# Graph attention, four layers on one core: elu and statistics on GpSimd, preparation spread over groups, stores apart

## The chip, the cores and the metric

The kernel runs on one core of one Trainium2 chip. The metric is the device time of one execution in microseconds, taken as the median of three: 2753.4 (2751.53 to 2755.9). Engines are named as in the profile: PE is TensorE, ACT is ScalarE, DVE is VectorE, POOL is GpSimd, SP issues most of the transfers.

## The reference

Sixteen batches of 1024 nodes with 256 features go through four layers of graph attention over one adjacency matrix. Each layer normalises its input, applies relu, projects it with W, and adds the attended result to x. Layers 0 and 2 have four heads of 64 features, layers 1 and 3 one head of 256. Layer 3 ends in relu, the others in elu.

```
h = maximum(layernorm(x), 0)            # eps 1e-5, over 256 features
Wh = h @ W                              # heads H, features D = 256 / H
e[i, j] = leaky_relu(Wh[i] . a_src + Wh[j] . a_dst)      # slope 0.2, layer 3: 0.01
alpha = softmax over j of (e where adj[i, j] > 0, else -inf)     # layers 2, 3: adj != 0
x = x + elu(alpha @ Wh)                 # layer 3: relu
```

All data are fp32.

## The kernel before

**The trick.** The exponential of a leaky relu of a sum is a maximum of two products of a factor of i and a factor of j. So no matrix of exponentials is computed. For a head, g is a row of 1024 factors of i, copied to all 128 partitions. One DVE instruction per 128 nodes j makes the tile w = max(g, rcol of j) x mask (L250, 128x1024, with g in PSUM and the mask as bytes in SBUF). TensorE multiplies w as the stationary operand with whx, the projected features scaled by the other factor, and a last column gives the softmax's divisor.

**Steps and groups.** The work is a list of 64 steps, each one layer on one batch (`order_of_steps`, L409). Four batches (streams) are under way at once and take turns, so that the next layer of a batch comes three or four steps later (two at the very end: step 61 is layer 2 of batch 15, step 63 its layer 3). A step has eight groups of aggregation. In a wide step (four heads) each head has eight tiles of w and two groups, each with four blocks of 128 nodes i. In a narrow step (one head) there are eight tiles in all, and each group has one block. `aggregate` (L254) emits a group's matmuls and one ACT copy of its PSUM sums to y (L270). PSUM has two buffers for these sums (`ps_acc`), two for g (`ps_g`), and two shared by transpositions and projections (`ps_p`).

**The order is written by hand.** From L387 on (`tc.manual_schedule()`) every engine gets its instructions in the order in which the Python program emits them. For group k of step n this is: the tiles that this head still lacks; the matmuls of the group and its y copy; pieces of the finish of step n-1 that are due; pieces of preparations that are due (`prepare`, L334); some tiles ahead (`emit_tiles`, L357): four per wide group, two per narrow one, never more than WBUFS = 19 beyond the last head that is done. The preparation of the first two steps stands ahead of this block (L383 to L385), where the framework's scheduler sets the order.

**Preparation of a step** (`preparation`, L149): statistics of 512 rows each (`stats`, twice: bn_stats and bn_aggr on DVE, then 1/sqrt and the shift on POOL), normalisation (`normalise`, four ACT copies each, twice), four transpositions (PE, then an ACT copy with relu), eight projections (two PE pairs each, three ACT copies; for wide layers a POOL product besides), the factors (`factors`, two ACT exponentials and a POOL minimum), and `rows`: a transposition of gcol, an ACT copy, and a transfer to DRAM. PREPARATION (L40) gives to each of these 18 pieces the group, counted from the start, in which it is due. A step's preparation starts two steps ahead, at group 0, or at group 4 where the last layer of the same batch is too near (L391).

**Tiles.** `fetch` (L236) reads a head's factors back from DRAM to all partitions (SP), `broadcast` (L242) copies them to PSUM on ACT (g), `weights` (L247) makes a tile. A head's g can be emitted once the whole preparation of its step has been emitted (`done["prepared"]`), and its place in ACT's queue is behind everything emitted before. If a step begins and its preparation isn't emitted yet, the rest of it is emitted on the spot (L362 to L367).

**Finish of a step** (`finish`, L272), in the next step: at group 0 the reciprocal of the divisor (DVE) and the scaling of the first half (POOL), at 1 that of the second half and the exponential of the first (ACT), at 2 and 3 the rest. `scaled` (L289) multiplies y and makes e = min(y, 0). `add` (L302) computes elu as max(e - 1, y) in one DVE instruction and adds it to x on POOL; in layer 3 one DVE instruction adds relu(y) to x, and the transfer of the half to DRAM is issued at once, with the load of the stream's next batch after the second. The tile e and the normalised tile xn share three buffers named t4.

Of the kernel before, what the change touches and what calls it, by code (L numbers as in the profile page):

```python
# [38 lines left out]
WBUFS = 19  # L39
PREPARATION = (0, 0, 1, 2, 3, 3, 4, 4, 5, 5, 5, 5, 6, 6, 7, 7, 8, 9)  # L40
# [11 lines left out]
def kernel(ctx: ExitStack, tc: tile.TileContext, x, adj, ws, avs, out):  # L52
# [96 lines left out]
    def preparation(n):  # L149
# [6 lines left out]
        def stats(half):  # L156
            if half == 0:
                st["mv"] = small.tile([P, C, 2], F32, name="mv")
                st["bn"] = small.tile([P, C, 6], F32, name="bn")
            for c in range(half * HALF, (half + 1) * HALF):  # L160
                nc.vector.bn_stats(st["bn"][:, c, :], xs[b][:, c, :])  # L161
                nc.vector.bn_aggr(st["mv"][:, c, :], st["bn"][:, c, :])  # L162
            if half == 1:
                rstd = st["rstd"] = small.tile([P, C], F32, name="rstd")
                nc.gpsimd.tensor_scalar(rstd, st["mv"][:, :, 1], EPS, None, op0=ALU.add)
                nc.gpsimd.tensor_tensor(rstd, rstd, neghalf, op=ALU.pow)  # L166
                shift = st["shift"] = small.tile([P, C], F32, name="shift")
                nc.gpsimd.tensor_tensor(shift, st["mv"][:, :, 0], rstd, op=ALU.mult)
                nc.gpsimd.tensor_scalar(shift, shift, -1.0, None, op0=ALU.mult)

        def normalise(half):
            xn = st["xn", half] = prep.tile([P, HALF, F], F32, name="t4", bufs=3)
# [61 lines left out]
        return list(zip(PREPARATION, out + [factors, rows], strict=True))  # L234
# [37 lines left out]
    def finish(n):  # L272
# [16 lines left out]
        def scaled(half):  # L289
# [3 lines left out]
            if l < L - 1:  # L293

                e = st["e", half] = prep.tile([P, HALF * H, D], F32, name="t4", bufs=3)
                nc.gpsimd.tensor_scalar(e, yh, 0.0, -3.0e38, op0=ALU.min, op1=ALU.max)  # L296
# [5 lines left out]
        def add(half):  # L302
            xh, yh, r = views(half)
            if l < L - 1:
                e = st["e", half]
                nc.vector.scalar_tensor_tensor(e, e, -1.0, yh, op0=ALU.add, op1=ALU.max)  # L306
                nc.gpsimd.tensor_add(xh, xh, e)  # L307
                return
            nc.vector.scalar_tensor_tensor(xh, yh, 0.0, xh, op0=ALU.max, op1=ALU.add)
            nc.sync.dma_start(  # L310
                out=out[b, half * HALF * P:(half + 1) * HALF * P, :].rearrange(
                    "(c p) f -> p c f", p=P), in_=xs[b][:, half * HALF:(half + 1) * HALF, :])
            if half == 1 and b + STREAMS < B:
# [4 lines left out]
                (2, lambda: add(0)), (3, lambda: add(1))]  # L318
# [12 lines left out]
    done = {"tiles": 0, "g": 0, "gs": 0, "free": 0, "prepared": 0, "wanted": 0}  # L331
    agenda = []

    def prepare(upto):  # L334

        while agenda and (agenda[0][0] <= upto or agenda[0][1] < done["wanted"]):
            _, n, piece, last = agenda.pop(0)
            piece()
            if last:
                done["prepared"] = n + 1  # L340
                fetch_heads()

    def plan(n, at):
# [101 lines left out]
```

## Time and profile before

The execution that was profiled took 2758.29 us, and its span, from the first instruction to the last, is 2756.5 us. That is 4.9 us over the median.

| what | us |
|---|---|
| median of three executions | 2753.4 |
| profiled execution | 2758.29 |
| its span | 2756.5 |
| matmuls of the aggregation (L266), busy | 1965.4 |
| matmuls of the projections (L195), busy | 515.8 |
| transpositions (L183), busy | 155.4 |
| tiles of w (L250), busy | 1543.3 |
| statistics bn_stats (L161), busy | 200.7 |

A group's row in the profile gives the line, the engine, the operation, the tiles written and read, their shapes, the number of instructions, then the busy time, the mean duration in ns, and the engine's idle time ahead of these instructions with what ended most of it. A line of waits gives who waited for whom: the sum in us, how often, and the longest. PEld is the load of stationary operands and runs beside PE; the ends of matmuls are modelled. Each L266 matmul stands in the trace as two records[...].

### The profile page before, as it was taken

What the parts mean: (1) busy time and instruction counts of PE and PEld (TensorE: products, weight loads), DVE (VectorE), ACT (ScalarE), POOL (GpSimd) and SP (SyncE); (2) the same over time, 40 slices, a digit from 0 to 9 for tenths busy, and PEclk for the clock granted to TensorE, in tenths of its full rate; (3) what the DMA queues carried; (4) which work ended last, traced back from release to release, by engine and by line L of the source; (5) the groups of instructions that cost most, each with busy time, mean ns of one, the idle gap of its engine ahead of it and who ended that gap; (6) DMA issues with size and microseconds to landing.
All of it is one profiled execution on the core that took longest, in us unless ns stands there. A gap on an engine that the chain in (4) does not pass through costs nothing.

```text
span 2756.5 us, 88771 instructions
## 1 busy us (share of the span) xinstructions
PE 2581.3 (94%) x40080; PEld 2268.5 (82%) x40080; DVE 1984.5 (72%) x2569; ACT 1199.6 (44%) x3265; POOL 896.6 (33%) x909
## 2 busy tenths in 40 slices
PE   1789988999999999999999999999999999999997
PEld 1688777888888888888888888888888888888876
DVE  5596855767966779747977679767797488775772
ACT  0534444444444444544444445444444444444341
POOL 0223333343332343342242343333323333433221
PEclk9999999999999999999999999999999999999998
DMA  4111010012211210111211111002112111101101
GB/s 138 62 49 40 10 40 25 25 36 67 72 36 44 71 49 25 41 39 47 88 41 48 62 40 41 33 17 71 56 49 71 34 46 64 34 17 39 56 25 39
DMA packets 63674, 130.08 MB, mean 47 GB/s; under 512 B 6208, under 2 KB 41792, under 8 KB 63296
## 3 DMA queue, kind: packets, MB, share of 16 engines
q1 hardware_dynamic: 60608, 123.35, 13.4%
q8 instruction: 315, 5.16, 0.8%
q10 hardware_dynamic: 2688, 1.05, 0.2%
q14 instruction: 63, 0.52, 0.1%
HBM read 106.95 MB, written 17.43 MB: 45 GB/s over the span
## 4 chain that ended last, share of the span: by engine, by line
PE 72%; DVE 14%; DMA 6%; ACT 4%; issue 3%; POOL 1%; DVEq 0%; ACTq 0%; SPq 0%; POOLq 0%
PE acc L266 53%; PE pp L195 15%; DVE w L250 11%; DMA gs<-grow 4%; PE pp L183 3%; DMA grow<-gT 2%; DVE bn L161 1%; ACT t L300 1%; ACT g L245 1%; DVE t L306 1%; DVE mv L162 1%; ACT whx L197 1%; DMA a_bc<-in_L_gnn_a 1%; ACT whx L201 0%; ACT y L270 0%
## 5 line engine op out<-in xcount | busy, mean ns | idle before, releaser
L266 PE MATMUL acc<-whx,w 128*64 128x65 f32 x36864 | 1965.4, 242 | 77.9 <-DVE w L250 56.9
L266 PEld LDWEIGHTS acc<-whx,w 128*64 128x64 f32 x36864 | 1764.3, 145 | 265.5 <-DVE w L250 78.7
L250 DVE SCALAR_TENSOR_TENSOR w<-g,rcol,mask 128x1024 f32<-128x1024 f32 x1280 | 1543.3, 1273 | 523.4 <-ACT g L245 432.7
L270 ACT ACTIVATE y<-acc 128x260 f32<-128x260 f32 (+1 forms) x512 | 196.8, 384 | 1071.1 <-PE acc L266 1069.8
L195 PE MATMUL pp<-wx,hT 128*128 128x258 f32 (+1 forms) x2048 | 515.8, 395 | 2.9 <-ACT hT L184 2.7
L291 POOL TENSOR_TENSOR y<-y,r 128x1024 f32<-128x1024 f32 x128 | 243.0, 1899 | 716.1 <-DVE r L287 716.1
L195 PEld LDWEIGHTS pp<-wx,hT 128*128 128x128 f32 x2048 | 378.3, 192 | 78.1 <-ACT hT L184 15.7
L307 POOL TENSOR_TENSOR x<-x,t 128x1024 f32<-128x1024 f32 x96 | 226.8, 2362 | 408.2 <-DVE t L306 399.6
L206 POOL TENSOR_TENSOR whx<-whx 128x256 f32<-128x256 f32 x256 | 157.5, 618 | 471.2 <-ACT whx L204 471.2
L175 ACT ACTIVATE t<-x,shift,rstd 128x256 f32<-128x256 f32 x512 | 264.8, 588 | 78.7 <-POOL x L307 56.6
L245 ACT ACTIVATE g<-gs 128x1024 f32<-128x1024 f32 x160 | 163.5, 1022 | 129.5 <-DMA gs<-grow 128.0
L197 ACT ACTIVATE whx<-pp,nbias 128x4 f32<-128x4 f32 (+1 forms) x512 | 135.5, 265 | 181.3 <-PE pp L195 169.7
L161 DVE BATCH_NORM_STATS2 bn<-x 128x6 f32<-128x256 f32 x512 | 200.7, 392 | 2.4 <-DMA x<-in_x 2.4
L183 PE MATMUL pp<-ident,t 128*128 128x128 f32 x1024 | 155.4, 284 | 34.0 <-ACT t L175 18.9
L183 PEld LDWEIGHTS pp<-ident,t 128*128 128x128 f32 x1024 | 111.3, 141 | 78.8 <-ACT whx L201 28.0
L184 ACT ACTIVATE hT<-pp 128x512 f32<-128x512 f32 x256 | 145.5, 593 | 19.2 <-PE pp L183 18.8
L306 DVE SCALAR_TENSOR_TENSOR t<-t,y 128x1024 f32<-128x1024 f32 x96 | 118.4, 1233 | 35.4 <-ACT t L300 35.3
L287 DVE RECIPROCAL r<-y 128x32 f32<-128x32 f32 (+1 forms) x64 | 17.6, 276 | 160.0 <-ACT y L270 159.9
L201 ACT ACTIVATE whx<-pp,whx 128x256 f32<-128x256 f32 x256 | 121.7, 475 | 0.0
L166 POOL TENSOR_TENSOR rstd<-rstd,neghalf 128x8 f32<-128x8 f32 x64 | 106.7, 1668 | 5.3
L162 DVE BATCH_NORM_AGGREGATE mv<-bn 128x2 f32<-128x6 f32 x512 | 92.8, 181 | 16.9
L296 POOL TENSOR_SCALAR t<-y 128x1024 f32<-128x1024 f32 x96 | 101.7, 1060 | 8.5
(37 smaller groups left out, 533.0 us busy)
## 6 DMA issues: line engine op xcount, KB each, us to landing
gs<-grow SPq DMA_DIRECT2D x160, 512.0 KB
x<-in_x SPq DMA_DIRECT2D x16, 1024.0 KB
out<-x SPq DMA_DIRECT2D x32, 512.0 KB
a_raw<-in_adj SPq DMA_DIRECT2D x8, 512.0 KB
a_bc<-in_L_gnn_a ACTq DMA_DIRECT2D x8, 128.0 KB
wx<-in_L_gnn_W SPq DMA_DIRECT2D x4, 256.0 KB
grow<-gT SPq DMA_DIRECT2D x32, 16.0 KB
grow<-gT SPq DMA_DIRECT2D x32, 4.0 KB
```

The source lines that it names most:

```text
L161: nc.vector.bn_stats(st["bn"][:, c, :], xs[b][:, c, :])
L175: nc.scalar.activation(xn[:, q, :], xs[b][:, c, :], AF.Identity, bias=st["shift"][:, c:c + 1], scale=st["rstd"][:, c:c + 1])
L183: nc.tensor.transpose(pt[:, q, :], st["xn", half][:, q, k * P:(k + 1) * P], ident)
L195: nc.tensor.matmul(pw, lhsT=st["hT", half][:, k, q * P:(q + 1) * P], rhs=wx[l][:, k, :], start=(k == 0), stop=(k == K - 1))
L197: nc.scalar.activation(whx[:, c, :, D], pw[:, F + H:F + 2 * H], AF.Exp, bias=nbias[l], scale=slope)
L206: nc.gpsimd.tensor_tensor(whx[:, c, :, 0:D], whx[:, c, :, 0:D], whx[:, c, :, D:D + 1].to_broadcast([P, H, D]), op=ALU.mult)
L245: nc.scalar.activation(g, state[n]["gs", h], AF.Copy)
L250: nc.vector.scalar_tensor_tensor(w, state[n]["g", h], state[n]["rcol"][:, jc, h:h + 1], masks[LAYERS[steps[n][1]][3]][:, jc, :], op0=ALU.m ...
L266: nc.tensor.matmul(acc[o % P:o % P + cols, q, :], lhsT=st["w", h, jc][:, o:o + cols], rhs=st["whx"][:, jc, h, :], start=(jc == 0), stop=(j ...
L270: nc.scalar.activation(st["y"][:, i0:i0 + per, h, :], acc, AF.Copy)
L291: nc.gpsimd.tensor_tensor(yh, yh, r[:, :, None].to_broadcast([P, HALF * H, D]), op=ALU.mult)
L307: nc.gpsimd.tensor_add(xh, xh, e)
```

## The change

The change has these parts:

- `stats` no longer calls bn_aggr. The means and squared deviations of the even and the odd elements that bn_stats leaves are combined for all 1024 rows at once by ten small POOL instructions (there were four).
- In `add`, elu's last step moves from DVE to POOL: y becomes max(y, 0) - 1, then e + y, then x + e.
- xn and e have buffers of their own, two each, and WBUFS goes from 19 to 18.
- A preparation has 20 pieces. Its last one does nothing but mark it as done, two groups after `rows` and the fetch of the first heads. PREPARATION spreads the pieces over 14 groups (it was 10). BEGIN and L394 to L402 of the new text give the start: two steps ahead, three groups earlier for wide steps; never before group 5 of the step in which the last layer of the same batch is finished (group 0 of the step after it for layer 0, whose x must be loaded first); and at least three groups after the one before it.
- The first two preparations are emitted inside the hand-written order.
- Where a preparation is late, the pieces of all steps that are due up to its end are emitted.
- In layer 3 both halves' stores, and the load after them, are issued at group 4 of the next step.

```diff
-WBUFS = 19
-PREPARATION = (0, 0, 1, 2, 3, 3, 4, 4, 5, 5, 5, 5, 6, 6, 7, 7, 8, 9)
+WBUFS = 18
+PREPARATION = (0, 1, 3, 4, 5, 5, 6, 6, 7, 7, 7, 7, 8, 8, 9, 9, 10, 11, 11, 13)
+BEGIN = {1: 0, 4: -3}
...
             for c in range(half * HALF, (half + 1) * HALF):
-                nc.vector.bn_stats(st["bn"][:, c, :], xs[b][:, c, :])
-                nc.vector.bn_aggr(st["mv"][:, c, :], st["bn"][:, c, :])
+                nc.vector.bn_stats(bn[:, c, :], xs[b][:, c, :])
             if half == 1:
+                m0, s0, m1, s1 = (bn[:, :, i] for i in (1, 2, 4, 5))
                 rstd = st["rstd"] = small.tile([P, C], F32, name="rstd")
-                nc.gpsimd.tensor_scalar(rstd, st["mv"][:, :, 1], EPS, None, op0=ALU.add)
+                nc.gpsimd.tensor_tensor(dev, m0, m1, op=ALU.subtract)
+                nc.gpsimd.tensor_tensor(dev, dev, dev, op=ALU.mult)
+                nc.gpsimd.tensor_scalar(dev, dev, 0.25, EPS, op0=ALU.mult, op1=ALU.add)
+                nc.gpsimd.tensor_tensor(rstd, s0, s1, op=ALU.add)
+                nc.gpsimd.tensor_scalar(rstd, rstd, 1.0 / F, None, op0=ALU.mult)
+                nc.gpsimd.tensor_tensor(rstd, rstd, dev, op=ALU.add)
                 nc.gpsimd.tensor_tensor(rstd, rstd, neghalf, op=ALU.pow)
...
-            xn = st["xn", half] = prep.tile([P, HALF, F], F32, name="t4", bufs=3)
+            xn = st["xn", half] = prep.tile([P, HALF, F], F32, name="xn")
...
-        return list(zip(PREPARATION, out + [factors, rows], strict=True))
+        out += [factors, rows, lambda: fetch_heads(n + 1), lambda: None]
+        return [(begin[n] + k, piece) for k, piece in zip(PREPARATION, out, strict=True)]
...
-                e = st["e", half] = prep.tile([P, HALF * H, D], F32, name="t4", bufs=3)
+                e = st["e", half] = prep.tile([P, HALF * H, D], F32, name="e")
...
-                nc.vector.scalar_tensor_tensor(e, e, -1.0, yh, op0=ALU.add, op1=ALU.max)
+                nc.gpsimd.tensor_scalar(yh, yh, 0.0, -1.0, op0=ALU.max, op1=ALU.add)
+                nc.gpsimd.tensor_add(e, e, yh)
                 nc.gpsimd.tensor_add(xh, xh, e)
                 return
             nc.vector.scalar_tensor_tensor(xh, yh, 0.0, xh, op0=ALU.max, op1=ALU.add)
+
+        def store(half):
             nc.sync.dma_start(
...
-                (2, lambda: add(0)), (3, lambda: add(1))]
+                (2, lambda: add(0)), (3, lambda: add(1))] + (
+                    [(4, lambda: store(0)), (4, lambda: store(1))] if l == L - 1 else [])
...
-                    done["wanted"] = n + 1
-                    prepare(-1)
+                    prepare(max(a[0] for a in agenda if a[1] == n))
...
+        begin.append(8 * (n - 2) + BEGIN[LAYERS[l][0]] if n > 1 else -99)
+        if b % STREAMS in last:
+            begin[n] = max(begin[n], 8 * (last[b % STREAMS] + 1) + (8 if l == 0 else 5))
+        if n > 2:
+            begin[n] = max(begin[n], begin[n - 1] + 3)
...
-    for n in range(2):
-        plan(n, -99)
-        prepare(0)
     ending = []
     with tc.manual_schedule():
+        for planned in (1, 2):
+            plan(planned - 1)
+            prepare(-1)
...
-                if n + 2 < len(steps) and k == (0 if ready_at[n + 2] < n - 1 else 4):
-                    plan(n + 2, 8 * n + k)
+                while planned < len(steps) and begin[planned] <= 8 * n + k:
+                    plan(planned)
+                    planned += 1
```

## The prediction, made before the changed kernel was run

> **What bounds the kernel now.** I read the page's busy times first, then the waits, then the stretches, one per step of the schedule. "Wide" is a step with four heads (32 tiles of w), "narrow" one with a single head (8 tiles); n.k is group k of step n. "T" is a transposition, "P" a projection; 16.3 means step 16, group 3.
>
> ```profile
> PE 2581.3 (94%) x40080; PEld 2268.5 (82%) x40080; DVE 1984.5 (72%) x2569; ACT 1199.6 (44%) x3265; POOL 896.6 (33%) x909
> ...
> L307 POOL TENSOR_TENSOR x<-x,t 128x1024 f32<-128x1024 f32 x96 | 226.8, 2362 | 408.2 <-DVE t L306 399.6
> ...
> L306 DVE SCALAR_TENSOR_TENSOR t<-t,y 128x1024 f32<-128x1024 f32 x96 | 118.4, 1233 | 35.4 <-ACT t L300 35.3
> ...
> L162 DVE BATCH_NORM_AGGREGATE mv<-bn 128x2 f32<-128x6 f32 x512 | 92.8, 181 | 16.9
> L296 POOL TENSOR_SCALAR t<-y 128x1024 f32<-128x1024 f32 x96 | 101.7, 1060 | 8.5
> ```
>
> TensorE is busy 94% of the span: 175 us of idle are all there is to win, and 64 of these lie in the first 100 us, before the matrices have arrived. The waits say what VectorE lacks:
>
> ```profile
> DVE w L250 <- ACT g L245: 432.7, 38, 26.9
> ...
> ACT t L175 <- POOL x L307: 56.6, 15, 5.0
> ```
>
> VectorE, at 72%, is idle for lack of a broadcast g, not of time. Now the steps, cut where the last y copy of each starts (columns: stretch, its length, then the busy us of PE, PEld, DVE, ACT, POOL):
>
> ```profile
> 382.40:432.10 49.70, 38.10 (x1034) 35.09 (x1033) 49.43 (x56) 14.61 (x31) 13.18 (x11) 0.93 0.08 24
> 477.60:530.70 53.10, 45.80 (x1074) 41.24 (x1074) 48.27 (x55) 21.45 (x53) 13.19 (x11) 0.94 0.07 23
> 814.00:855.30 41.30, 41.09 (x1074) 37.79 (x1074) 38.56 (x46) 18.75 (x51) 6.37 (x7) 1.00 0.20 67
> 1051.40:1096.20 44.80, 41.89 (x1074) 38.23 (x1074) 42.57 (x50) 19.54 (x52) 16.88 (x17) 1.00 0.05 15
> ```
>
> They are the wide steps 6, 8, 16 and 22. Step 16 is entered with 12 tiles made, and TensorE never waits. Steps 6 and 8 are entered with six, and VectorE, busy all through step 6, sets the pace: 49.7 and 53.1 us. So the time is decided by how many tiles exist when a wide step begins. Floors, the shortest steps in this cut: wide 41.2, narrow 37.6. Steps 9 to 59 take 2056.9 together, 49 over their floors. What a step costs when it is entered with nothing stands near the end:
>
> ```profile
> 2657.76 0.27 PE L223 MATMUL pp<-ident,gcol 128*8 128x128 f32 x1
> ...
> 2658.17 0.25 ACT L225 ACTIVATE gT<-pp 8x128 f32<-8x128 f32 x1
> ...
> 2658.44 0.30 SPq L227 DMA_DIRECT2D grow<-gT  x1
> 2659.74 0.34 SPq L239 DMA_DIRECT2D gs<-grow  x1
> 2663.87 1.03 ACT L245 ACTIVATE g<-gs 128x1024 f32<-128x1024 f32 x1 [3.49 <-DMA gs<-grow]
> ...
> 2664.94 9.63 DVE L250 SCALAR_TENSOR_TENSOR w<-g,rcol,mask 128x1024 f32<-128x1024 f32 x8 [7.16 <-ACT g L245]
> ```
>
> From the transposition of the factors to the eighth tile: 16.8 us. Tiles stand 1.20 apart (9.63 for eight).
>
> **What the Trainium skill says.** "GPSIMD Engine Reference", 4.1 Engine selection: two-input elementwise work is about twice as slow on GpSimd, one-input work about line rate. The trace agrees: 2362 ns for L307 against 1233 for L306, and 1060 for the one-input L296. "SBUF — State Buffer", SBUF: two separate sides: GpSimd and VectorE exclude each other only where VectorE reads two SBUF operands or is in a two-port mode; w takes g from PSUM, so I give it no penalty, and its pitch in this trace is 1.20 in busy and idle stretches of GpSimd alike. "Perfetto Trace Analysis", Tensor Engine Instruction: ScalarE, VectorE and GpSimd are strict FIFO. That decides here: a g behind a y copy waits for TensorE.
>
> **The change, part by part.**
>
> Engines. VectorE loses 96 L306 (118 us) and 512 L162, of which a step shows a pitch of 0.53 per chunk going to 0.40: 1.1 us per step, 3.6 with the two L306. GpSimd gains per half one one-input operation (1.06) and one two-input (at most 2.36): 96 x 3.4 = 328 us, and six tiny ones per step (0.2 to 0.25, pitch 0.3): 1.8 x 64 = 115. It comes to some 1340 us, 48%. Its chain after a step is 2 x 2.95 (scale, clamp) + 2 x 5.8 (elu, add) = 17.5 us, plus 4.4 of statistics; x is complete some 24 us into the next step, while the earliest statistics of a wide step follow at group 5, 29 or more us in. I take 0 for it; if the cover is gone, see the rivals. That xn and e have buffers of their own takes the 56.6 us off ScalarE; behind them stand y copies, and TensorE's share is the 0.4 to 1.4 us by which narrow steps exceed 37.6. It is inside the 49.
>
> Spreading. The last piece of a preparation now lies 13 groups after its start, and g may be broadcast only after it. Counting the order of instructions: wide steps of layer 0 (16, 19, 21, 32, 35, 37, 48, 51, 53) start their preparation at group 0 two steps before, so the first g comes at group 5 of the narrow step ahead, not at group 1, and six tiles are issued before they begin. Wide steps of layer 2 keep 12. In steps 3, 5, 6, 8, 62 and 63 the preparation isn't over when the step begins: the rest is issued on the spot, ahead of its first matmul.
>
> (a) Start. The first two preparations now come under the written order. In the trace the first g (96.50) runs before the second preparation is done; in the new order of ScalarE it follows all of it. One preparation alone: eight normalisations (4.1) and the rest as in the trace from hT (74.2) to the factors' transposition (88.6), some 14. Statistics are ready 1.7 later (six more tiny operations). So 72.0 + 18 = 90, 108 for the second, gT and g: first w at 110 in place of 97.6, +12.5. Through step 1 VectorE is the bound: two L306 (2.4), half of step 3's statistics moved behind the last needed tile (2.6) and the missing aggregations (1) return 6. Net +6.
>
> (b) Steps 2 to 8. A forced entry in detail, step 6: after the last matmul of step 5, two P and two T stand ahead of the factors' transposition (3.8), then 16.8 to the eighth tile: 20.6. TensorE has P and T for 7.2 and its first group's 3.8 meanwhile: 10 lost. Then 24 tiles and half of the statistics, 28.8 + 1.6, set the end of step 6: 51 for the last tile, 7 more for its groups, 58. By the same working, a head's first group held until its eighth tile, steps 2 to 8 take 52.8, 45.6, 48.8, 56.0, 58.0, 42.6, 61.3 = 365.1; in the trace they are 50.6, 38.0, 42.2, 51.1, 49.7, 45.5, 53.1 = 330.2. Some 5 us of projections are put off beyond step 8 as well. +40.
>
> (c) Steps 9 to 59. Work only moves between neighbours; stalls count. Step 16: its first eight tiles are made as it begins; 24 more, a whole set of statistics (3.2), r, and about 2 us in which g stands behind a normalisation bring the last at 34.1. Without stalls TensorE needs it at 28.9 (six groups of 3.82, P and T 5.1, a quarter group): 5.3. Step 19 has another half of statistics ahead: 6.9. Step 21 has two sets, its first eight tiles come 2.8 late (g at 20.5 stands behind two P), and only 6 us of P and T lie in it: last tile at 37.6 against 25: 12.6. Sum 24.8 per round of 16 steps; three rounds and steps 14, 30 and 46 (1.5 each: they keep 12 tiles) make 79; less the 49 now: +30.
>
> (d) Steps 60 to 63. In the trace step 63 starts its preparation at 61.4, ahead of the finish of step 61 on the same batch; now at 62.5, after it. Step 62: 1.6 (y, factors) + 16.8 + 0.5 = 18.9 for a group of 3.5, so 43.3 with seven more. Step 63: normalisation to factors, with nothing beside it, 18.3; then 16.8 and a last pair: 35.8 + 24.4 = 60.2. Step 60 holds no P now (28.2), step 61 as before (40.8). 172.5 against 157.8, with 2 us of P moved ahead: +17. The last stores only change their place in SP's queue: 0; those of the other batches come one group later, still four groups, some 18 us, ahead of the next statistics of that stream: 0.
>
> Sum: 6 + 40 + 30 + 17 = +93 on the profiled 2758.3 (span 2756.5 and 1.8 around it). That execution is 4.9 over the median, so 2753.4 + 93 = 2846.
>
> **Rivals.** (1) Tiles suffice: the nine layer-0 entries cost 2 each, since step 16's last tile is only 5 behind and the 2 us of g and part of the rest may vanish; 79 becomes 22, total +36: 2789. For it: VectorE's 28% idle. Against: steps 6 and 8. (2) Faster: VectorE's relief decides. If the eight tiles of a forced entry were ready in the 11 us that TensorE still has work, not after 20, (a) and (b) would give 0, the 3.6 us would take 45 of the 49, the end would cost 17: 2725. Against: the 7.2 us from transposition to first tile are one row of DMA and copies that the change doesn't shorten. (3) GpSimd becomes the bound: statistics of a wide step, two groups after the elu, wait in VectorE's queue with all tiles behind them; 3 us at 28 wide steps is +84 on top: 2930. For it: 5.8 us per half in place of 3.6 (1.2 + 2.4); against: a margin of about 5 us and 52% idle.
>
> **How the numbers follow.** Forecast 0.63 (own range 2816 to 2876), rival 1 0.20, rival 2 0.07, rival 3 0.08, nothing to tell (within 0.2%, about what a measurement of this kernel can tell) 0.02. The range 2770 to 2890 holds the forecast and rival 1, and leaves out rivals 2 and 3. Unknown costs: elu operations 0 to +84, entries 2 to 9 each, start +3 to +10. Faster 0.07, same 0.02, slower 0.91.
>
> **What would show it.** First w near 110 us; about 20 us without accumulation ahead of steps 3, 5, 6, 8, 62 and over 30 ahead of 63; wide steps 16, 19, 21 at 46 to 50 us with VectorE busy throughout; VectorE down to about 1775 busy, GpSimd near 1340; no wait of L175's line for x. It would be wrong if those wide steps stay at 41 us, or if the statistics wait for GpSimd's x.

## The result: 6.2% slower, 77 us more than forecast

The changed kernel takes 2923.4 us, median of four executions (2921.1 to 2929.7), against 2754.7 us for the kernel before (2751.5 to 2756.4) on the same chip. The ratio is 1.0617, with a 95% interval of 1.0598 to 1.0637. The forecast was 2846, in a range of 2770 to 2890: the right sign, and a time outside the range.

Cut as in the prediction, where the last y copy of each step starts, the two profiled executions compare as follows. The forecast column adds the working on record to the stretch before.

| stretch | before | forecast | after | difference, forecast | difference, measured |
|---|---|---|---|---|---|
| steps 0 and 1 | 200.4 | 206.4 | 207.6 | +6 | +7.2 |
| steps 2 to 8 | 330.3 | 365.1 | 369.1 | +40 (5 of it later) | +38.8 |
| steps 9 to 59 | 2056.9 | 2086.9 | 2154.5 | +30 | +97.6 |
| steps 60 to 63 | 157.7 | 172.5 | 176.7 | +17 (2 of it earlier) | +19.0 |

The last column adds up to the difference of the spans (2918.9 less 2756.5) within 0.2 us. The forecast put 7 us of projections, which (b) and (d) count, into the middle. In the traces 24 records of projections move there, some 6 us (steps 2 to 8 have 233 of them in place of 249, steps 60 to 63 have 64 in place of 72). Counted like the forecast, (a) is 7 us for 6, (b) 43 for 40 and (d) 21 for 17. Term (c), the long middle, is 92 for 30, three times what was said. So the question is what happens in steps 9 to 59.

The page's busy times of the kernel after, then rows of its groups (line, engine, operation, tiles, shapes, count, then busy us, mean ns and the idle time before):

```profile
PE 2636.9 (90%) x40080; PEld 2310.4 (79%) x40080; DVE 1790.9 (61%) x1961; ACT 1209.5 (41%) x3265; POOL 1529.1 (52%) x1485
```

```profile
L319 POOL TENSOR_SCALAR y<-y 128x1024 f32<-128x1024 f32 x96 | 348.9, 3634 | 3.4
...
L320 POOL TENSOR_TENSOR e<-e,y 128x1024 f32<-128x1024 f32 x96 | 209.2, 2179 | 24.7 <-ACT whx L208 16.0 <-ACT e L313 1.4
...
L309 POOL TENSOR_SCALAR e<-y 128x1024 f32<-128x1024 f32 x96 | 99.8, 1040 | 8.5
```

VectorE is down to 1791 us, as forecast (1775). GpSimd stands at 1529 in place of 1340, and one row shows why: elu's max/add (L319) takes 3634 ns. The forecast gave it 1.06 us, from the row of the other one-input operation on the same shape (L309, 1040 ns here).

The waits of the kernel after, in the whole span (who waits for whom: us in total, times, longest):

```profile
DVE w L263 <- ACT g L258: 948.9, 97, 49.6
...
PE acc L279 <- DVE w L263: 126.0, 126, 7.8
DVE bn L164 <- POOL x L321: 81.7, 14, 16.0
...
PE pp L234 <- POOL gcol L229: 48.7, 20, 7.2
```

VectorE now waits 949 us for a broadcast g; before it was 433. It has less to do and gets its work later. Of the last two lines the first is new: statistics wait for GpSimd's x, which the forecast had named as a sign that it would be wrong. The other wait has grown from 3.0 us: TensorE itself stands before the transposition of the factors (L234) until GpSimd has taken their minimum (L229).

How that second wait arises is seen in step 15, in the order of time (start, us, engine, line, operation, then in brackets the idle time and who ended it):

```profile
840.86 0.31 ACT L227 ACTIVATE gcol<-sd,rbias 128x32 f32<-128x32 f32 x1
...
841.36 3.63 POOL L319 TENSOR_SCALAR y<-y 128x1024 f32<-128x1024 f32 x1
845.07 2.16 POOL L320 TENSOR_TENSOR e<-e,y 128x1024 f32<-128x1024 f32 x1
847.32 2.34 POOL L321 TENSOR_TENSOR x<-x,e 128x1024 f32<-128x1024 f32 x1
849.74 0.29 POOL L229 TENSOR_SCALAR gcol<-gcol 128x32 f32<-128x32 f32 x1
...
850.09 0.39 PE L234 MATMUL pp<-ident,gcol 128*32 128x128 f32 x1 [7.22 <-POOL gcol L229]
...
860.77 1.04 ACT L258 ACTIVATE g<-gs 128x1024 f32<-128x1024 f32 x1
861.84 8.43 DVE L263 SCALAR_TENSOR_TENSOR w<-g,rcol,mask 128x1024 f32<-128x1024 f32 x7 [35.45 <-ACT g L258]
```

The factors are ready at 841.17. A minimum of 0.29 us stands behind one half of elu in GpSimd's queue, and starts 8.6 us later. TensorE does nothing for 7.2 us before the transposition, since the aggregation stands behind it in TensorE's queue. And g for the wide step 16, which begins at 868.9, reaches VectorE after 35 us without work.

The steps 15, 16, 19, 21 and 22 of the kernel after (stretch, its length, then the busy us of PE, PEld, DVE, ACT, POOL, then TensorE's granted clock, the share of the DMA engines and GB/s):

```profile
822.10:868.90 46.80, 39.34 (x178) 33.40 (x179) 11.36 (x17) 17.68 (x50) 29.50 (x27) 0.93 0.11 35
868.90:916.70 47.80, 44.63 (x1075) 40.76 (x1074) 44.35 (x45) 19.57 (x52) 7.53 (x13) 0.93 0.21 69
991.50:1039.00 47.50, 43.64 (x1074) 39.70 (x1074) 44.53 (x51) 21.07 (x54) 29.32 (x30) 0.96 0.10 35
1085.70:1133.90 48.20, 39.66 (x1042) 36.96 (x1040) 45.92 (x52) 15.73 (x33) 29.53 (x31) 0.89 0.14 47
1133.90:1184.50 50.60, 48.71 (x1106) 43.32 (x1107) 37.35 (x32) 25.54 (x74) 27.31 (x19) 1.00 0.07 24
```

Steps 16, 19 and 21 are at 47.5 to 48.2 with VectorE busy nearly throughout, inside the 46 to 50 that was forecast. Step 15, a narrow one of which nothing was forecast, takes 46.8 where it took 38.7. A second thing stands in the clock column: 0.89 to 0.96 in four of these five steps, where the middle of the kernel before had 1.00 nearly everywhere.

### The profile page after: what moved, and what is told of

It reads as the page before. It is cut to its first block, busy times and chain, and to the rows that moved or that the text cites. A ratio compares the mean times of both kernels' runs of the same rounds, so it can differ in the third digit from the quotient of the medians.

```text
span 2918.9 us, 89625 instructions
## 1 busy us (share of the span) xinstructions
PE 2636.9 (90%) x40080; PEld 2310.4 (79%) x40080; DVE 1790.9 (61%) x1961; ACT 1209.5 (41%) x3265; POOL 1529.1 (52%) x1485
## 3 DMA queue, kind: packets, MB, share of 16 engines
q10 hardware_dynamic: 2688, 1.05, 0.2%
## 4 chain that ended last, share of the span: by engine, by line
PE 68%; DVE 14%; POOL 7%; issue 5%; ACT 4%; DMA 2%; DVEq 0%; POOLq 0%; ACTq 0%; SPq 0%
PE acc L279 50%; PE pp L206 14%; DVE w L263 12%; PE pp L194 3%; POOL y L319 2%; DVE bn L164 1%; POOL x L321 1%; POOL e L320 1%; ACT xn L186 1%; ACT whx L208 1%; POOL rstd L177 1%; DMA gs<-grow 1%; ACT g L258 1%; ACT whx L212 1%; DMA a_bc<-in_L_gnn_a 0%
## 5 line engine op out<-in xcount | busy, mean ns | idle before, releaser
L279 PE MATMUL acc<-whx,w 128*64 128x65 f32 x36864 | 2018.5, 246 | 131.0 <-DVE w L263 126.0
L263 DVE SCALAR_TENSOR_TENSOR w<-g,rcol,mask 128x1024 f32<-128x1024 f32 x1280 | 1541.6, 1274 | 965.2 <-ACT g L258 948.9
L279 PEld LDWEIGHTS acc<-whx,w 128*64 128x64 f32 x36864 | 1805.4, 148 | 332.7 <-DVE w L263 170.1
L319 POOL TENSOR_SCALAR y<-y 128x1024 f32<-128x1024 f32 x96 | 348.9, 3634 | 3.4
L186 ACT ACTIVATE xn<-x,shift,rstd 128x256 f32<-128x256 f32 x512 | 263.7, 589 | 13.4 <-POOL shift L180 13.4
L321 POOL TENSOR_TENSOR x<-x,e 128x1024 f32<-128x1024 f32 x96 | 227.1, 2365 | 7.5
L164 DVE BATCH_NORM_STATS2 bn<-x 128x6 f32<-128x256 f32 x512 | 174.7, 407 | 84.4 <-POOL x L321 81.7
L320 POOL TENSOR_TENSOR e<-e,y 128x1024 f32<-128x1024 f32 x96 | 209.2, 2179 | 24.7 <-ACT whx L208 16.0
L194 PE MATMUL pp<-ident,xn 128*128 128x128 f32 x1024 | 157.4, 285 | 39.7 <-ACT xn L186 24.1
L194 PEld LDWEIGHTS pp<-ident,xn 128*128 128x128 f32 x1024 | 112.5, 142 | 84.6 <-ACT xn L186 28.5
L258 ACT ACTIVATE g<-gs 128x1024 f32<-128x1024 f32 x160 | 163.7, 1024 | 13.4 <-DMA gs<-grow 13.3
L195 ACT ACTIVATE hT<-pp 128x512 f32<-128x512 f32 x256 | 146.0, 595 | 22.2 <-PE pp L194 21.3
L229 POOL TENSOR_SCALAR gcol<-gcol 128x32 f32<-128x32 f32 (+1 forms) x64 | 20.2, 315 | 200.7 <-ACT gcol L227 198.5
```

Of the source, the lines that this page charges most:

```text
L164: nc.vector.bn_stats(bn[:, c, :], xs[b][:, c, :])
L186: nc.scalar.activation(xn[:, q, :], xs[b][:, c, :], AF.Identity, bias=st["shift"][:, c:c + 1], scale=st["rstd"][:, c:c + 1])
L194: nc.tensor.transpose(pt[:, q, :], st["xn", half][:, q, k * P:(k + 1) * P], ident)
L258: nc.scalar.activation(g, state[n]["gs", h], AF.Copy)
L263: nc.vector.scalar_tensor_tensor(w, state[n]["g", h], state[n]["rcol"][:, jc, h:h + 1], masks[LAYERS[steps[n][1]][3]][:, jc, :], op0=ALU.m ...
L279: nc.tensor.matmul(acc[o % P:o % P + cols, q, :], lhsT=st["w", h, jc][:, o:o + cols], rhs=st["whx"][:, jc, h, :], start=(jc == 0), stop=(j ...
```

## Experiments

Fourteen kernels were run. Times are medians of four executions; each ratio is to the kernel before, run on the same chip, with its 95% interval. Comparisons between runs go by these ratios.

| run | what differs | us | ratio |
|---|---|---|---|
| after | the change | 2923.4 | 1.0617 [1.0598, 1.0637] |
| e1 | after, elu on VectorE | 2901.2 | 1.0531 [1.0513, 1.0548] |
| e4 | after, minimum of the factors on VectorE | 2963.4 | 1.0755 [1.0739, 1.0772] |
| e5 | e1 with TensorE's gaps filled | 2891.5 | 1.0512 [1.0496, 1.0528] |
| e9 | after, elu on GpSimd in other forms | 2908.4 | 1.0566 [1.0550, 1.0582] |
| e10 | after, layer-0 preparation 3 groups earlier | 2815.8 | 1.0229 [1.0214, 1.0245] |
| e14 | after, layer-0 preparation 2 groups earlier | 2830.4 | 1.0287 [1.0272, 1.0302] |
| e13 | e10, elu on VectorE | 2823.7 | 1.0254 [1.0234, 1.0274] |
| e11 | after, pieces at the old pace | 2857.8 | 1.0377 [1.0360, 1.0394] |
| e3 | before, elu on GpSimd | 2838.2 | 1.0302 [1.0287, 1.0318] |
| e6 | before, buffers of their own | 2771.1 | 1.0077 [1.0061, 1.0092] |
| e7 | before, all of the change but its order | 2724.8 | 0.9907 [0.9892, 0.9921] |
| e8 | e7, elu in other forms | 2711.9 | 0.9862 [0.9846, 0.9879] |
| e12 | e8, step 63 prepared after step 61's addition | 2735.6 | 0.9937 [0.9922, 0.9953] |

The fourteenth kernel, m1, measures operations alone.

### What makes the operation of elu long (m1)

```diff
+ts(f, yv, 0.0, -3.0e38, op0=ALU.min, op1=ALU.max)   # L79
+ts(zv, yv, 0.0, -3.0e38, op0=ALU.min, op1=ALU.max)  # L80
+ts(yv, yv, 0.0, -1.0, op0=ALU.max, op1=ALU.add)     # L81
...
+ts(f, e, 0.0, -1.0, op0=ALU.max, op1=ALU.add)       # L84
...
+ts(f, e, 0.5, -1.0, op0=ALU.mult, op1=ALU.add)      # L87
+ts(f, e, 0.0, None, op0=ALU.max)                    # L88
...
+ts(yv, yv, 0.0, 3.0e38, op0=ALU.max, op1=ALU.min)   # L91
```

Here ts is GpSimd's tensor_scalar, yv and zv are strided views like the one of y in the kernel, and e and f are contiguous. The line numbers are added here.

> A kernel that computes nothing of the reference: it leaves out all of the work and runs forms of GpSimd's tensor_scalar on 128 x 1024 float32, three of each, to find what makes max/add 3.63 us where min/max is 1.04 us. If the pair of operations decides, every max/add takes about 3.6 us, contiguous or not, in place or not, and min/max takes 1.04 us even when it writes the strided tile. If the strided output or working in place decides, max/add from contiguous to contiguous takes about 1.04 us, and min/max into the strided tile about 3.6 us.

Groups of this kernel on GpSimd:

```profile
L81 POOL TENSOR_SCALAR y<-y 128x1024 f32<-128x1024 f32 x3 | 10.9, 3634 | 0.3
L91 POOL TENSOR_SCALAR y<-y 128x1024 f32<-128x1024 f32 x3 | 10.9, 3625 | 0.2
...
L84 POOL TENSOR_SCALAR f<-e 128x1024 f32<-128x1024 f32 x3 | 10.9, 3624 | 0.2
...
L88 POOL TENSOR_SCALAR f<-e 128x1024 f32<-128x1024 f32 x3 | 8.3, 2772 | 0.2
...
L80 POOL TENSOR_SCALAR z<-y 128x1024 f32<-128x1024 f32 x3 | 3.5, 1162 | 7.9 <-DVE z L74 7.8
L87 POOL TENSOR_SCALAR f<-e 128x1024 f32<-128x1024 f32 x3 | 3.1, 1045 | 0.2
L79 POOL TENSOR_SCALAR f<-y 128x1024 f32<-128x1024 f32 x3 | 3.1, 1038 | 0.2
```

The pair of operations decides, not the layout: max/add takes 3.63 us strided and in place, and 3.62 from contiguous to contiguous. Two pairs take a third of that: min/max (1.04) and mult/add (1.05). The 1.16 of min/max into the strided tile (L80) is a mean of one at 1.41 and two at 1.04; in e8 and e9 below, min/max on the strided y takes 1.04 too. Turned round to max/min, the same two operations take 3.63, and a single max takes 2.77. So the forecast's 1.06 was the price of a pair that happened to be one of the two cheap ones among the five that were measured.

### Elu's place in the change (e1, e4, e9)

```diff
-                nc.gpsimd.tensor_scalar(yh, yh, 0.0, -1.0, op0=ALU.max, op1=ALU.add)
-                nc.gpsimd.tensor_add(e, e, yh)
+                nc.vector.scalar_tensor_tensor(e, e, -1.0, yh, op0=ALU.add, op1=ALU.max)
```

> The changed kernel with the last step of elu back on VectorE as one scalar_tensor_tensor per half (1.23 us on VectorE) in place of max/add (3.63 us) and the two-input add (2.18 us) on GpSimd; everything else of the change stays. Theory A (the forecast costed elu's GpSimd operations too small and took nothing for what stands behind them in GpSimd's queue; the schedule costs what was forecast): GpSimd falls to about 970 us busy, the two waits of TensorE for the factors' minimum (48.7 and 54.8 us) and the wait of the statistics for x (81.7 us) go, and the time falls by 50 to 75 us, to about 2850 to 2870. Rival B (the new order of the preparation costs nearly all of the 169 us; elu's place does not matter): within 15 us of 2923.

The measured 2901.2 is 22 us below the change. Neither side of the expectation holds: TensorE's wait for the minimum shrinks from 48.7 to 15.8 us and the statistics' wait for x from 81.7 to 5.6, but the gain is less than half of the least that Theory A hoped for. Elu on GpSimd costs something, and it isn't the main thing.

e4 moves the small operation alone:

```diff
-            nc.gpsimd.tensor_scalar(gcol, gcol, EXP_SHIFT, None, op0=ALU.min)
+            nc.vector.tensor_scalar(gcol, gcol, EXP_SHIFT, None, op0=ALU.min)
```

> The changed kernel with one operation moved: the minimum over the factors (0.24 or 0.39 us) on VectorE in place of GpSimd. Theory A1 (of what elu costs, most passes through this minimum: TensorE's transposition of the factors stands behind it in TensorE's order, 48.7 us of wait at the transposition and 54.8 at its weight load, the same waits seen twice): 35 to 50 us faster than the changed kernel, 2873 to 2888. Rival A2 (what costs is that x is late and the statistics hold VectorE, 81.7 us of wait): less than 20 us faster, or slower if the minimum then waits behind tiles in VectorE's queue.

It is 40 us slower than the change. VectorE's queue is the worse place: the minimum holds back the tiles behind it until the exponential has come. The trace has 556.6 us of VectorE idle at this line in 60 waits, while its wait for g falls from 948.9 to 458.3. Rival A2 had this possibility in it. What TensorE's wait for the minimum costs this run doesn't tell: that wait goes (6.9 us are left), but a new one takes its place.

e9 shortens elu with the forms of m1:

```diff
-                nc.gpsimd.tensor_scalar(yh, yh, 0.0, -1.0, op0=ALU.max, op1=ALU.add)
+                nc.gpsimd.tensor_scalar(yh, yh, 3.0e38, 0.0, op0=ALU.min, op1=ALU.max)
+                nc.gpsimd.tensor_scalar(e, e, 1.0, -1.0, op0=ALU.mult, op1=ALU.add)
                 nc.gpsimd.tensor_add(e, e, yh)
```

> The changed kernel with elu's last step on GpSimd as min/max (1.16 us), mult/add (1.05) and the addition (2.18), 4.4 us per half in place of 5.8, with the same values. The run with elu on VectorE gave 22 us; the forecast took 3.4 us per half as free. If the length of these operations is what costs in this order, two thirds or more of the 22 come back: 2898 to 2910; if the factors' minimum behind them in GpSimd's queue were the main loss of steps 9 to 59, more: 2860 to 2890.

It takes 2908.4 us, in the range of the first theory: by the ratios 14 of the 24 us that e1 gains come back with the length of the operations.

### The other half of the square: all but the order (e3, e6, e7, e8)

e3 puts only the two lines of elu into the kernel before.

> The kernel before with nothing changed but elu's last step: max/add and the two-input add on GpSimd in place of the one operation on VectorE. Theory A: GpSimd's chain after a step grows by 9.2 us in all (two halves of 4.6), x comes later and small operations wait in its queue here too; slower than the kernel before by 20 to 70 us, 2775 to 2825. Rival B: within 10 us of 2754, or a little faster, since VectorE loses 118 us of work.

It is 84 us slower, above Theory A's 20 to 70. In this kernel the normalisation shares its three buffers with e. Its wait for x grows with elu's length; it was 56.6 us before:

```profile
ACT t L175 <- POOL x L308: 155.0, 40, 6.1
```

Own buffers alone were not added to this run, so how much of the 84 us this wait costs stays open.

e6 gives xn and e buffers of their own, and nothing else:

```diff
-WBUFS = 19
+WBUFS = 18
-            xn = st["xn", half] = prep.tile([P, HALF, F], F32, name="t4", bufs=3)
+            xn = st["xn", half] = prep.tile([P, HALF, F], F32, name="xn")
-                e = st["e", half] = prep.tile([P, HALF * H, D], F32, name="t4", bufs=3)
+                e = st["e", half] = prep.tile([P, HALF * H, D], F32, name="e")
```

> The kernel before with one part of the change alone: xn and e in buffers of their own, two each, in place of three shared ones, and 18 buffers of w in place of 19. Theory: the wait of the normalisation for x (56.6 us in 15 waits) goes, TensorE's share of it is small: 2735 to 2754. Rival: 18 buffers of w hold VectorE back at the wide steps: slower by 5 to 20.

It is 20 us slower: most wide steps go from 41.3 to 42.5. The theory falls, and the rival's size fits; whether it is the 18 buffers of w wasn't tried apart. Something else can be read here. The wait of 56.6 us is gone, and the narrow steps are as long as before: the 26 of steps 9 to 59 exceed 37.6 us by 23.0 together, before by 21.9. The forecast had put this excess down to that wait.

e7 takes buffers, statistics and elu together, and leaves the order out:

> The kernel before with all parts of the change but its order: buffers of their own, statistics combined on GpSimd, elu's last step on GpSimd as in the changed kernel (3.63 and 2.18 us); the preparation keeps the old pace, and the stores their old place. Theory B1 (elu on GpSimd costs 84 us in the kernel before because xn waits for buffers that e holds until x is added, and about 20 with buffers of its own): 2750 to 2790, and the order is then worth 130 to 170 of the 169. Rival B2 (elu's price is GpSimd's queue itself): 2810 to 2845, and the order is worth about 80 to 110.

It takes 2724.8 us, below both theories and 26 us below the kernel before (ratio 0.9907). With elu's last step and bn_aggr off VectorE, its 1791 us of work no longer hold back the wide steps: step 22 falls from 44.8 to 42.0, and statistics hardly wait for x (7.6 us in 3). So the same operations that were suspected make the kernel faster in the old order. The new order, the place of the stores included, costs 1.0617 less 0.9907, 7.1% or 195 us. e8 has the short forms in it:

> As the run before it, but elu's last step on GpSimd as min/max (1.16 us), mult/add (1.05) and the addition (2.18): 4.4 in place of 5.8 us per half, with the same values. Under B1 it gains little, 0 to 20 us on the run before it; under B2 24% of elu's price, 15 to 25 us. Below 2740 it would beat the kernel before: VectorE then has 118 us less to do in an order whose wide steps begin with 12 tiles.

It takes 2711.9 us, 1.4% below the kernel before and 13 us below e7, in the range of B1.

### Which part of the order (e10, e11, e14)

One number of the new planner:

```diff
-            begin[n] = max(begin[n], 8 * (last[b % STREAMS] + 1) + (8 if l == 0 else 5))
+            begin[n] = max(begin[n], 8 * (last[b % STREAMS] + 1) + (5 if l == 0 else 5))
```

> The changed kernel with one number changed: the preparation of a layer-0 step starts 5 groups after the end of the last step on its stream, not 8. By the order of the instructions its nine wide steps (16, 19, 21 and repetitions) then begin with 12 tiles, like the wide steps of layer 2. The forecast's term (c) put 5.3, 6.9 and 12.6 us on these entries, 74 in three rounds: 60 to 75 us faster than the changed kernel, 2848 to 2863, steps 16 and 19 at 41 to 42 us. Forecast's rival 1 (tiles suffice, 2 us each): 2895 to 2910. Theory E (the entry is one cause of several: GpSimd's queue and VectorE's own pace take their place): 2870 to 2895.

It takes 2815.8 us: 108 us are gone, more than the forecast's own 74. Steps 9 to 59 take 2046.7, 10 less than before the change; the other stretches stay (372.0 and 175.8 for steps 2 to 8 and 60 to 63). All that the middle lost hangs on this number. Steps 15, 16 and 21 of this kernel, in the columns of above:

```profile
826.90:857.60 30.70, 30.70 (x146) 26.73 (x147) 18.70 (x23) 13.89 (x31) 25.94 (x21) 1.00 0.22 70
857.60:898.90 41.30, 41.08 (x1074) 37.78 (x1073) 33.20 (x38) 18.65 (x50) 7.55 (x13) 1.00 0.22 67
...
1061.60:1097.70 36.10, 34.32 (x1042) 32.84 (x1041) 35.72 (x43) 15.78 (x34) 27.20 (x27) 1.00 0.16 59
```

Step 16 is at its floor, and TensorE is at full clock in all three. Steps 15 and 21 are under the floors of the prediction, because projections and transpositions now stand in other steps (step 15 has 146 matmul records, in the kernel after 178); so only sums over many steps can be held against the floors. What TensorE waited for in steps 9 to 59, first after the change, then in e10:

```profile
PE acc L279 <- DVE w L263: 46.3, 60, 0.9
PE pp L234 <- POOL gcol L229: 41.3, 15, 7.2
```

```profile
PE acc L279 <- DVE w L263: 17.0, 31, 0.9
...
PE pp L234 <- POOL gcol L229: 0.5, 2, 0.3
```

The wait for the minimum goes and the one for tiles falls to a third, though elu still runs on GpSimd with its 3.63 us. The start decides where the factors' minimum stands in GpSimd's queue: with 8 it falls into group 2 of steps 15, 31 and 47, behind elu's addition (7.2 us each, 21.7 of the 41.3), and into group 2 of steps 20, 36 and 52 (2.3 us each); with 5 it stands in group 7 of the step before, clear of it. The statistics' wait for x remains (82.8 us against 81.7; in steps 9 to 59 it is 22.3 against 22.2, none longer than 4.5), and so it isn't what start 5 saves. In exchange the statistics now wait for the load of the stream's next batch, 50.2 us in 12 waits in these steps.

e14 takes 6:

> The changed kernel with 6 in place of 8 (5 gave 2815.8): by the order of the instructions the nine wide layer-0 entries have one pair of tiles less than with 5, and the factors come at the beginning of steps 15, 31 and 47, no longer behind elu's additions of group 2. Theory H (the number of tiles at the entry decides, by degrees): between, 2835 to 2880. Rival I (the collision with elu is what counts, entries little): within 15 us of 2816.

It takes 2830.4 us, just under the range of H and at the edge of I. Two groups bring 93 of the 108 us of steps 9 to 59 (2061.1), the third 14. The price isn't in proportion to the tiles missing at the entry.

e11 keeps the starts and gives the pieces their old pace:

```diff
-PREPARATION = (0, 1, 3, 4, 5, 5, 6, 6, 7, 7, 7, 7, 8, 8, 9, 9, 10, 11, 11, 13)
+PREPARATION = (0, 0, 1, 2, 3, 3, 4, 4, 5, 5, 5, 5, 6, 6, 7, 7, 8, 9, 9, 9)
```

> The changed kernel with the old offsets of the preparation's pieces (0 to 9, both markers at 9), begun when the change begins it: what the spreading over 13 groups costs. By the order of the instructions all wide steps but the first ones begin with 12 tiles, and only step 63 is entered by force. The forecast's terms: 74 of (c), nearly all of (b)'s 40 and some 6 of (d) go: 2790 to 2815. If the time of the starts is what counts and not the spreading: 2870 or more. Left over would be the start of the kernel and step 63, some 25 to 35 us on the run of 2724.8.

It takes 2857.8 us, 43 us above the first range that was expected and 12 below the other. Steps 16, 19 and 21 are at their floors (41.1, 41.0, 39.7), and steps 2 to 8 take 346.7, so that of the 39 us there 22 belong to the spreading. But the narrow steps lose: TensorE is idle for 3.0, 3.0 and 3.2 us in steps 23, 26 and 28, where the change has none, and in the whole span the normalisation waits 91.5 us for the statistics from GpSimd (13.4 in the change). At the old pace the normalisation comes right behind the statistics, and their ten small operations on GpSimd take 4.2 us in a row (837.2 to 841.4 in step 15 of the kernel after). But the statistics in their turn wait longer for x here (111.2 us against 81.7), and e7, which has the same pace, loses nothing by it. So which of the two costs these gaps, and what else lies in the remaining difference from e7, wasn't taken apart.

### Elu's price, with the order right (e13)

e13 is e10 with the diff of e1; it closes the square.

> The run of 2815.8 us (layer-0 preparation begun 5 groups after the end of the stream's last step, not 8) with elu's last step on VectorE; with the changed kernel (8, GpSimd: 2923.4), the run of 2901.2 (8, VectorE) and that of 2815.8 (5, GpSimd) the fourth of a square. Theory F (elu on GpSimd costs 22 us only where the factors' minimum falls right behind it in GpSimd's queue, which start 8 brings about and start 5 does not): no gain, 2810 to 2840, the more the 118 us count that VectorE gets back. Rival G (its length costs in any order, the two prices simply add): 2788 to 2800.

It takes 2823.7 us: no gain, 0.25% above e10, with intervals that just overlap. So it comes out as Theory F said: with start 5, elu on GpSimd costs nothing. Steps 9 to 59 give the square in us. Each figure is from one execution, and executions of one of these kernels differ by 5 to 9 us. These steps are 25 wide and 26 narrow ones, and the floors on record make 25 x 41.2 + 26 x 37.6 = 2007.6:

| | elu on GpSimd | elu on VectorE |
|---|---|---|
| start 8 | 2154.5 | 2130.6 |
| start 5 | 2046.7 | 2052.7 |

That it is the minimum through which elu costs time with start 8 is read from the waits. In these steps TensorE waits for it 41.3 us in the kernel after, 25.6 in e9, 8.3 in e1 and 0.5 in e10, and the steps get 14 us shorter from the kernel after to e9 and 24 to e1. No run takes this wait away alone; the statistics' wait for x falls with it (22.2 us in the kernel after, 12.1 in e9, none in e1). With start 5, though, its going brings nothing: it is 22.3 in e10 and none in e13.

### Is it TensorE's clock? (e5)

In the trace's clock record the kernel before has 16 stretches at half clock, 71 us, and the changed one 33, 234 us. Each of these is 3.41 us or a multiple of it but for one in each kernel, which the end cuts off. The sum of matmul time in steps 9 to 59 rises from 2013 to 2050 us for nearly the same work (31,460 records in place of 31,428). So the suspicion was that each gap costs twice. e5 puts useless products into the gaps of 15 places:

```diff
+    FILL = {(16, 2): 5, (19, 2): 5, (21, 1): 6, (21, 2): 4, (22, 2): 4}
...
+            for _ in range(FILL[at, h]):
+                nc.tensor.matmul(pd, lhsT=ident, rhs=wx[0][:, 0, :], start=True, stop=True)
```

> The changed kernel with elu on VectorE (the run of 2901.2 us), and with four to six matrix products of no use (0.39 us each) put in TensorE's queue ahead of the first group of the head at which steps 16, 19, 21, 22 and their repetitions wait for tiles: 15 places, 12 of them with a stretch of half TensorE clock behind the gaps, 9 stretches of 6.83 us and 3 of 3.41. Theory C (each stall costs twice: the gap, and then 3.41 us or a multiple at half clock; the forecast priced the gap alone): the half clock goes at these places and the time falls by 20 to 35 us, to 2866 to 2881, although TensorE has 28 us more to do. Rival D (VectorE's pace sets the end of these steps, so the clock behind the gap costs nothing): within 6 us of 2901, or slower by up to 28.

The middle of step 16, in stretches of 2 us, first e1 and then e5 (columns as above):

```profile
890.00:892.00 2.00, 0.67 (x8) 0.40 (x8) 2.00 (x3) 2.00 (x4) 0.00 (x0) 0.98 0.21 29
892.00:894.00 2.00, 0.75 (x8) 0.56 (x10) 2.00 (x3) 0.26 (x1) 0.00 (x0) 0.50 0.94 248
894.00:896.00 2.00, 2.00 (x42) 2.00 (x42) 2.00 (x3) 0.00 (x0) 0.00 (x0) 0.50 1.07 381
```

```profile
890.00:892.00 2.00, 1.71 (x28) 1.16 (x26) 2.00 (x2) 1.88 (x3) 0.00 (x0) 1.00 0.35 76
892.00:894.00 2.00, 0.98 (x26) 0.84 (x28) 2.00 (x3) 0.00 (x0) 0.00 (x0) 1.00 0.96 265
894.00:896.00 2.00, 2.00 (x76) 2.00 (x74) 2.00 (x3) 0.00 (x0) 0.00 (x0) 1.00 1.08 383
```

The half clock is gone there (21 stretches are left in all, 166 us), and the time isn't: 2891.5 against 2901.2, and by the ratios 1.0512 against 1.0531, whose intervals overlap. Step 16 takes 47.3 in place of 47.5, step 21 46.4 for 47.4 and step 22 51.7 for 53.3. VectorE is busy in every microsecond of both fences; TensorE, faster now, waits for later tiles instead. Theory C falls, with its 20 to 35 us. In these steps the slow clock is a sign that TensorE lacks tiles, and at most a small part of the price.

### The end (e12)

In the kernel before, step 63's statistics and normalisation stand in the program ahead of step 61's addition to the same x: the last normalisation starts at 2666.6, the last addition to x at 2691.4. So layer 3 of batch 15 is normalised from an x that still lacks what layer 2 adds. The change puts them behind. e7 and e8 do as the kernel before. e12 does the same in e8:

```diff
+                if n + 1 < len(steps) and ready_at[n + 1] == n - 1 and k == 4:
+                    plan(n + 1, 8 * n + k)
```

> The run of 2711.9 us (old order, buffers of their own, statistics and elu on GpSimd in the fast forms) with one step of the order moved: the preparation of step 63 starts at group 4 of step 62, behind step 61's addition to the same x, as in the changed kernel, not at group 4 of step 61, ahead of it. By the forecast's term (d) this costs 15 to 25 us: 2727 to 2737, still faster than the kernel before. If more than that is lost at the end, over 2750.

It takes 2735.6 us, in the range. By the ratios this order costs 0.75%, 21 us, and steps 60 to 63 take 171.4 us in place of 155.7. So term (d) is mostly the price of having x complete (16 of the 19 us). With it, this version is 0.6% faster than the kernel before and 6.4% faster than the changed one (0.9937 against 1.0617).

## Why the forecast was right in three terms and wrong in the fourth

**(a), (b) and (d).** First w: forecast 110, measured 112.9. Steps 2 to 8, forecast one by one, came within 2.1 us each: the first 52.8 for 53.0 measured, the last 61.3 for 62.2. The working behind them, from the last matmul of a step over the factors' transposition to the eighth tile, holds. The same chain is seen at the end, in steps 62 and 63 of the kernel after:

```profile
2801.59 0.27 PE L234 MATMUL pp<-ident,gcol 128*8 128x128 f32 x1 [1.19 <-POOL gcol L229]
2807.28 1.03 ACT L258 ACTIVATE g<-gs 128x1024 f32<-128x1024 f32 x1 [5.11 <-DMA gs<-grow]
2808.34 9.63 DVE L263 SCALAR_TENSOR_TENSOR w<-g,rcol,mask 128x1024 f32<-128x1024 f32 x8 [20.23 <-ACT g L258]
...
2832.77 1.41 DVE L164 BATCH_NORM_STATS2 bn<-x 128x6 f32<-128x256 f32 x4 [14.55 <-POOL x L321]
2841.05 1.41 DVE L164 BATCH_NORM_STATS2 bn<-x 128x6 f32<-128x256 f32 x4 [6.87 <-POOL x L321]
```

From 2801.59 to the end of the eighth tile, 2817.97, are 16.4 us; 16.8 were forecast. The two waits for x at the end are where elu's length does show in (d): step 63 took 64.7, 60.2 were forecast, and 60.3 are measured with elu on VectorE (e1).

**(c).** The forecast said: 24.8 us a round at the three layer-0 entries, in three rounds 74.4, and 1.5 each at steps 14, 30 and 46; together 79 over the floors, less the 49 that the kernel before has over them. Measured are 141 over the floors (2154.5 less 2007.6, less the 6 of moved projections, which (b) and (d) count). The square divides them:

| part of steps 9 to 59 | forecast | measured | from |
|---|---|---|---|
| late start of the layer-0 preparation | 74.4 | 77.9 | 2130.6 less 2052.7, both with elu on VectorE |
| stalls left with the early start | 4.5 | 39.1 | 2052.7 less 2007.6, less the 6 |
| elu on GpSimd with start 8 | 0 | 23.9 | 2154.5 less 2130.6 |

The first line, the reasoning the forecast was most at pains with, is right to 4 us in its sum. By entries there is luck in it: the forecast gives steps 16, 19 and 21 5.3, 6.9 and 12.6 over the floor, e1 has 6.3, 6.6 and 6.2, and the rest lies in steps next to them (step 22 takes 53.3 in e1 and 48.7 in e13). Rival 1, in which tiles suffice, falls with it. With elu on GpSimd the late start costs 107.8, because there the two prices meet.

The second failed in the step "less the 49 now". Subtracting all 49 says that every stall of the kernel before goes away and only the named ones come. The one reason given was the excess of the narrow steps, which e6 contradicts. What TensorE waits for in steps 9 to 59, first before, then in e13:

```profile
PE acc L266 <- DVE w L250: 15.5, 24, 0.9
PE acc L266 <- ACT y L270: 14.9, 17, 1.2
PE pp L183 <- ACT whx L204: 6.1, 26, 0.2
PE pp L183 <- ACT whx L201: 5.4, 25, 0.2
```

```profile
PE acc L279 <- DVE w L263: 22.3, 35, 0.9
PE pp L194 <- ACT whx L215: 6.1, 26, 0.2
PE pp L194 <- ACT whx L212: 5.6, 26, 0.2
```

These are all but 2 us of TensorE's idle time there (43.9 us before, 36.1 in e13). Only the wait for y copies is gone. The transpositions wait for ScalarE's copies of the projections as before (11.7 us for 11.5), which no part of the change touches, and the wait for tiles is longer. So 39 us stay of the 49. Why tiles are short in e13 wasn't taken apart.

The third failed twice: "one one-input operation (1.06)", which is 3.63, and "I take 0 for it", with a cover of the statistics alone in view. In step 15 x is complete 36 us into the step (858.4 less 822.1) and not 24, and still the statistics had room in most of the middle. What hadn't, by the waits, was the factors' minimum, an operation of 0.3 us in the same queue, which stands ahead of TensorE. Rival 3 named GpSimd, but with another victim: the wait of the statistics that it priced is as long in e10, which is 108 us faster. That its 2930 is close to the 2923 measured is an accident.

The three lines fall short by 3.5, 34.6 and 23.9, together the 62 us by which (c) was short. The other 8 of the 70 us between the sum of +93 and the spans are small misses of (a), (b) and (d), all to the same side.

On the pages: "GPSIMD Engine Reference" of the Trainium skill, 4.1 Engine selection, has one-input work on GpSimd at about line rate. The measurement agrees for min/max and mult/add, and contradicts it for max/add (3.63 against 1.04 on the same shape), so the measurement decides. "TensorE: Matmul & The Clock Gate", What's actually happening, describes a half clock that is set by windows of about 3.4 us, and was not used in the forecast. The trace agrees on the length (3.41 and multiples). As e5 shows, where 68 us less of half clock changed the time by 0.2%, leaving it out wasn't the error.

## What to carry to other kernels

An operation is priced by a row with the same operation on the same engine, not by one with the same number of inputs; where no row has it, its range is carried into the sum, and so is everything behind it in that engine's queue, above all a small operation for which TensorE waits. When stalls are counted over a floor, the old ones stay in the sum until a reason takes each of them out. And when one part of a change looks guilty, it is to be tried in the old surroundings too: elu and statistics on GpSimd with buffers of their own were worth 26 us of gain, and the new order hid it with 195 us of loss, 108 of them from one number in the planner.

## What the runs showed of the hardware that was not expected

- GpSimd's tensor_scalar on 128x1024 float32 (m1): 1.04 us for min then max and 1.05 for mult then add, 3.62 to 3.64 for max then add, add then max, and max then min, 2.77 to 2.78 for a single max or a single add. Written as times 1, plus -1 (e8, e9), the addition of -1 takes 1.05 us in place of the 2.77 of a single add.
- TensorE's clock was halved although TensorE was never idle for even 1 us at a time. In e1 it was busy from 884.0 us without a gap until 889.6, then in two bursts of 0.34 us at a pitch of 1.19, idle for at most 0.86 us between; a stretch of 6.83 us at half clock began at 891.9.
